# A sparse graph-attention kernel: masks only on slots that may be empty, one look at the sums per layer, and 272 slots in place of 277

## The chip, the cores and the metric

The kernel runs on one core of one Trainium2 chip. The metric is the device time in microseconds from the start to the end of one execution, as a median over several runs. A core has five engines that work through their own queues of instructions and wait for one another by semaphores: PE (TensorE, matrix products; its weight loads are shown apart as PEld), DVE (VectorE, elementwise work and reductions), ACT (ScalarE, activations and copies), POOL (GpSimd, here mostly the issue of indirect DMAs) and SP (here plain DMAs). Sixteen DMA engines carry out the transfers.

## The reference

Four layers of graph attention work on the same graph: 2048 nodes, 8 batches, 128 features. The adjacency matrix is random with a density of 1/128, so a node has 16 neighbours in the mean. Cut to what matters:

```python
x = normal((8, 2048, 128)); adj = bernoulli(0.0078125, (2048, 2048))

# layers 0 and 1, 8 heads of 16
scores = einsum('bnhd,bmhd->bhnm', Q, K) / sqrt(16)
scores = where(adj == 0, -inf, scores)
attn_out = einsum('bhnm,bmhd->bnhd', softmax(scores), V)
x = layer_norm(h + attn_out @ Wo + bo)
x = layer_norm(x + relu(x @ W1 + b1) @ W2 + b2)

# layers 2 and 3
h = x @ W
e = leaky_relu((h @ a_src)[:, :, None] + (h @ a_dst)[:, None, :], 0.2)
att = softmax(where(adj == 0, -inf, e))
x = layer_norm(att @ h + x)
```

All of it is in float32.

## The kernel before

**Tiles and slots.** The kernel does not compute the 2048 x 2048 scores. On the chip it finds each node's list of neighbours, ranks the nodes by falling degree, and cuts the ranked nodes into 16 blocks of 128, one node per partition. Block t has a fixed number of slots, `CAPS[t]` (line 41): slot s of a block holds, for each of its 128 nodes, that node's s-th neighbour. Since the nodes are ranked, block 0 needs many slots and block 15 few. Block 0 has `BASE` = 28 ordinary slots and `FOLD` = 2 folded ones: in a folded slot the 128 partitions serve the first `MANY` = 16 nodes eight times over, so these 16 nodes have 28 + 16 slots. The caps sum to 277. A node that has fewer neighbours than its block has slots leaves some of its slots empty; an empty slot's index points at row 2048 of the table, which a gather skips in layers 0 and 1 (out of bounds) and reads as a row of zeros in layers 2 and 3.

**A layer.** The rows of a table in HBM hold, per node, the keys and values of all batches (layers 0 and 1, 8 KB) or the projected features and two exponentials per batch (layers 2 and 3, 4160 bytes). For each slot POOL issues one indirect gather of 128 rows (`gather`, L284). Slots are worked on in chunks: of up to two slots in layers 0 and 1, up to four in layers 2 and 3. `pieces` (line 63) cuts the blocks into chunks evenly and sets their order; seven buffers hold chunks, and `fetch` issues the gathers of a chunk four or five chunks ahead of the one in work.

**A chunk of layers 0 and 1** (`attention_chunk`) goes through these steps. DVE multiplies the gathered keys by the queries (L600) and adds pairs of products (L606). PE turns the sums round with eight transposes that accumulate in PSUM (L291, tile `pair`), so that slots and heads lie on partitions. For each slot, one more matmul adds the mask (L613): its stationary operand is the column of `lmask` for that slot, broadcast to 64 columns, which holds -1e30 for nodes where the slot is empty and 0 elsewhere; its moving operand is a bfloat16 identity. ACT takes the exponential (L620) into one of eight places of `ring`. PE turns the weights back (L624), ACT copies them (L628), DVE multiplies the values by them (L636), and PE adds the products into `acc` by transposing them (L291, tile `acc`), eight matmuls per slot.

**Sums of weights.** When a block's last chunk is through the exponential, `block_sums` adds all its exponentials by matmuls (L580), ACT copies the result (L585, tile `sums`, 128 x 64) and takes its logarithm, from which the scale of the block's output is made. The `sums` function then has DVE reduce the copy to its least and greatest value (L648, L649), into `dmin` and `dmax`, one column per layer and block.

**Tails.** After a block's last chunk its tail runs beside the next block's chunks: output projection, two layer norms, the feed-forward network, and the projection into the next layer's table (L688 to L731, L488), all on PE and ACT. The blocks get shorter towards the end of a layer while a tail stays the same.

**A chunk of layers 2 and 3** (`gat_chunk`) multiplies small vectors for the weights (L764, L765, L770), scales seven of eight batches of features on DVE (L776) and the eighth on ACT (L781), in layer 2 adds one pair of slots on DVE (L787), and adds up on PE (L291). It uses no mask: an empty slot's row is zero.

**Order of the work.** The program is written under a manual schedule: `layers` walks over the list of chunks and calls the steps of neighbouring chunks in a fixed interleaving (a chunk's value product comes up to three chunks after its key product), and generators in `threads` and `tails` are advanced between them. Each engine runs its queue in that order.

**The check at the end.** `find_lists` (L325 to L366) makes the lists, `lmask`, and one number per node in `over`: the entry just past the block's last slot (L340), which is zero if all neighbours fitted. `verdict` reduces `dmin`, `dmax`, `over` and the scores of layers 2 and 3 to one flag. If a neighbour list did not fit, or sums were out of range, the flag makes the program run `general_path` after it, a dense computation of all four layers. The profile of the kernel before shows no instruction of that path.

The functions that the diff touches:

Of the kernel before, what the change touches and what calls it, by code (L numbers as in the profile page):

```python
# [8 lines left out]
F32 = mybir.dt.float32  # L9
# [5 lines left out]
ALU = mybir.AluOpType  # L15
AX = mybir.AxisListType
# [20 lines left out]

BASE, MANY, FOLD = 28, 16, 2  # L40
CAPS = [BASE + FOLD, 23, 21, 20, 19, 18, 18, 17, 16, 16, 15, 14, 14, 13, 12, 11]

# [41 lines left out]
def sparse_path(ctx: ExitStack, tc: tile.TileContext, ins: dict, out: bass.AP, flag: bass.AP):  # L86
# [81 lines left out]
    found = dram.tile([N, N // SEG * 8], F32, name="found")  # L168
    dmin = const.tile([P, 4, NT], F32, name="dmin")
    dmax = const.tile([P, 4, NT], F32, name="dmax")  # L170

# [148 lines left out]
    def find_lists(t):  # L322

        every = work.tile([P, N // SEG * 8], F32, tag="cand", name="cand", bufs=3)
        nc.gpsimd.indirect_dma_start(  # L325
            out=every, out_offset=None, in_=found,
            in_offset=bass.IndirectOffsetOnAxis(ap=perm[:, t : t + 1], axis=0),
        )
        for _ in range(12):
            yield  # L330
        s = CAPS[t] if t > 0 else BASE + FOLD * (P // MANY)
        rounds = s // 8 + 1
        top = small.tile([P, 48], F32, tag="top", name="top")
        for r in range(rounds):
            nc.vector.max(top[:, 8 * r : 8 * r + 8], every)
            if r + 1 < rounds:
                nc.vector.match_replace(every, top[:, 8 * r : 8 * r + 8], every, 0.0)
            if r % 3 == 2:
                yield
        nc.vector.tensor_copy(over[:, 1, t : t + 1], top[:, s : s + 1])  # L340
        if t == 0:
            few = small.tile([P, 1], F32, tag="few", name="few", bufs=1)
            nc.vector.tensor_single_scalar(few, node[:, 0:1], float(MANY), op=ALU.is_ge)
            nc.vector.scalar_tensor_tensor(
                over[:, 1, 0:1], top[:, BASE : BASE + 1], few, over[:, 1, 0:1],
                op0=ALU.mult, op1=ALU.max,
            )
            pf = misc()[:, : s - BASE]
            nc.tensor.matmul(pf, spread, top[:, BASE:s], start=True, stop=True)
            own = small.tile([P, P // MANY, FOLD], F32, tag="own", name="own", bufs=1)  # L350
            nc.vector.tensor_mul(
                own, pf.rearrange("p (g i) -> p g i", i=FOLD),
                group[:, :, None].to_broadcast([P, P // MANY, FOLD]),
            )
            s = CAPS[0]
            nc.vector.tensor_reduce(
                top[:, BASE:s], own.rearrange("p g i -> p i g"), axis=AX.X, op=ALU.add
            )
        sl = slice(first[t], first[t] + s)
        nc.vector.tensor_scalar(lmask[:, sl], top[:, :s], 0.0, NEG, op0=ALU.is_equal, op1=ALU.mult)  # L360

        far = small.tile([P, 48], F32, tag="far", name="far")
        nc.vector.tensor_scalar(
            far[:, :s], top[:, :s], 0.0, float(N + 1), op0=ALU.is_equal, op1=ALU.mult
        )
        nc.vector.scalar_tensor_tensor(  # L366
            lists[:, sl], top[:, :s], -1.0, far[:, :s], op0=ALU.add, op1=ALU.add
        )
        yield
# [200 lines left out]
    def block_sums(l, t, box, last):  # L570

        assert written[0] - box["exps"][0][2] < RING
        terms = [(e, fold_slots[: e.shape[0], :]) for e, folded, _ in box["exps"] if not folded]
        if "partial" in box:
            terms.append((ident, box["partial"]))
        if last and t == 0:
            terms += [(merge, box["wf"][:, i, :]) for i in range(FOLD)]
        ps = misc()[:, : NB * NH]
        for i, (a, b) in enumerate(terms):
            nc.tensor.matmul(  # L580
                ps, a, b, start=i == 0, stop=i + 1 == len(terms), skip_group_check=True
            )
        name = "sums" if last else "partial"
        box[name] = small.tile([P, NB * NH], F32, tag=name, name=name)
        nc.scalar.copy(box[name], ps)  # L585
        box["exps"].clear()
        if last:
            box["r"] = small.tile([P, NB * NH], F32, tag="logs", name="logs", bufs=1)
            nc.scalar.activation(box["r"], ps, AF.Ln)
            threads.append(scales(l, box))  # L590

    def attention_chunk(l, c):
# [17 lines left out]
        for j in range(NH):  # L610
            turn_into(sc, hk[:, j, :], j == 0)
        for i in range(ns):
            nc.tensor.matmul(  # L613
                sc[i * NB * NH : (i + 1) * NB * NH, :],
                lmask[:, at + i : at + i + 1].to_broadcast([P, NB * NH]), ident_bf,
                start=False, stop=True, skip_group_check=True,
            )
# [27 lines left out]

    def sums(l, t, box):
        if l < 2:
            nc.vector.tensor_reduce(dmin[:, l, t : t + 1], box["sums"], axis=AX.X, op=ALU.min)  # L648
            nc.vector.tensor_reduce(dmax[:, l, t : t + 1], box["sums"], axis=AX.X, op=ALU.max)  # L649
            return  # L650
        box["r"] = reciprocal_sums(l, t, box["w"], NB, box.get("folded"))

# [1111 lines left out]
```

## Time and profile before

| | |
|---|---|
| median of 3 runs | 2881.68 us (2877.71 to 2886.89) |
| profiled execution | 2878.0 us, of which the span from first to last instruction is 2876.1 us |
| mean granted TensorE clock | 0.94 of full speed |
| finding lists and the first table | 0 to 150 us |
| layer 0 | 150 to 1165 us |
| layer 1 | 1165 to about 1955 us |
| layer 2 | to about 2435 us |
| layer 3 | to the end |
| HBM | 937.16 MB read, 91.55 MB written |
| gathers (L284) | 1108, of 277 slots in four layers |
| masks (L613) | 554, of 277 slots in two layers |
| chunks | 142 in layers 0 and 1 each, 75 in layers 2 and 3 each |

The profile shows one execution. A group of instructions is shown as: line, engine, operation, the tile written and the tiles read, shapes, how often; then, after a bar, the busy time in us and the mean duration in ns; after a second bar, how long the engine stood idle just ahead of these instructions and what ended that idle time. "DVE ... <-ACT weights L628" says that DVE waited until ACT's instruction of line 628 had written `weights`. A table of stretches gives, for each stretch of the span, the busy time and the number of instructions of each engine, then the granted TensorE clock, the mean busy share of the 16 DMA engines and the GB/s that they moved. In a timeline a row is: start in us, busy us, engine, line, and how many instructions were merged into it.

### The profile page before, as it was taken

How to read it: one execution, taken by the hardware profiler on the slowest of the kernel's cores; microseconds unless marked ns; L12 is line 12 of the kernel's file. 1: busy time of each engine (PE TensorE's matmuls, PEld its weight loads, DVE VectorE, ACT ScalarE, POOL GpSimd, SP SyncE). 2: the span in 40 equal slices, each digit the busy share in tenths (PEclk: the TensorE clock that was granted, in tenths of full speed). 3: DMA queues.
4: the chain of work that ended last, by engine and by line, in shares of the span. 5: the costliest groups of instructions: out<-in, count | busy, mean ns of one | idle time of the engine just before them, and what ended most of it. 6: DMA issues, size and time to landing. Idle time of an engine off the chain costs nothing.

```text
span 2876.1 us, 51147 instructions
## 1 busy us (share of the span) xinstructions
PE 2456.2 (85%) x18834; PEld 2217.1 (77%) x18834; DVE 2559.8 (89%) x2563; ACT 1383.4 (48%) x5035; POOL 1778.6 (62%) x1297
## 2 busy tenths in 40 slices
PE   5867899899999999699989999998577787787786
PEld 4656788788888888688888888887567786777786
DVE  8888999999999888899899999996889997698996
ACT  3511444454455554154444555556345565354454
POOL 1267688688657544655566565553777775577773
PEclk9978999999999999899999999999789888999998
DMA  9698899999989878789899999976999998899995
GB/s 359 247 367 326 351 332 350 367 329 348 378 322 359 296 278 350 269 313 349 336 371 357 349 362 354 335 285 222 355 411 400 407 405 333 307 411 412 411 412 210
DMA packets 200684, 987.57 MB, mean 343 GB/s; under 512 B 31916, under 2 KB 33708, under 8 KB 128432
## 3 DMA queue, kind: packets, MB, share of 16 engines
q0 software_dynamic: 175024, 890.45, 80.6%
q1 hardware_dynamic: 20502, 75.52, 6.8%
q10 hardware_dynamic: 4900, 18.24, 1.6%
q8 instruction: 152, 2.49, 0.3%
q14 instruction: 106, 0.87, 0.1%
HBM read 937.16 MB, written 91.55 MB: 358 GB/s over the span
## 4 chain that ended last, share of the span: by engine, by line
PE 47%; DVE 22%; DMA 11%; issue 8%; ACT 6%; POOL 1%; POOLq 0%; DVEq 0%; ACTq 0%
PE acc L291 16%; DMA kv<-table,lists 8%; DVE kv L600 7%; DVE kv L636 7%; PE pair L291 4%; PE m L731 4%; PE m L710 4%; PE m L488 3%; PE m L298 3%; DVE kv L776 2%; DMA kv<-table,sorted_lists 2%; PE m L726 2%; PE m L580 2%; PE m L539 2%; DVE kv L606 2%
## 5 line engine op out<-in xcount | busy, mean ns | idle before, releaser
L284 POOL DMA_INDIRECT kv<-table,lists x955 | 1324.0, 1386 | 685.8 <-PE acc L291 303.3
L291 PE MATMUL acc<-ident,kv 128*128 128x128 f32 x8208 | 1080.9, 286 | 157.7 <-DVE kv L636 71.1
L291 PEld LDWEIGHTS acc<-ident,kv 128*128 128x128 f32 x8208 | 981.2, 148 | 220.6 <-DVE kv L636 81.9
L600 DVE TENSOR_TENSOR kv<-kv,q 128x2048 f32<-128x2048 f32 (+1 forms) x282 | 628.9, 2230 | 59.6 <-DMA kv<-table,lists 28.3
L636 DVE TENSOR_TENSOR kv<-kv,weights 128x2048 f32<-128x2048 f32 (+1 forms) x284 | 636.9, 2242 | 47.5 <-ACT weights L628 47.5
L776 DVE TENSOR_TENSOR kv<-kv,pair 128x3584 f32<-128x3584 f32 (+1 forms) x150 | 540.0, 3600 | 1.0
L291 PE MATMUL pair<-ident,kv 128*128 128x128 f32 (+1 forms) x2272 | 303.6, 278 | 79.5 <-issue 58.5
L606 DVE TENSOR_TENSOR kv<-kv 128x1024 f32<-128x1024 f32 (+1 forms) x284 | 340.3, 1198 | 9.2
L291 PEld LDWEIGHTS pair<-ident,kv 128*128 128x128 f32 (+1 forms) x2272 | 260.2, 142 | 97.6 <-issue 71.9
L781 ACT ACTIVATE kv<-kv,ws 128x128 f32<-128x128 f32 x554 | 177.6, 397 | 174.7 <-DVE ws L770 169.7
L284 POOL DMA_INDIRECT kv<-table,sorted_lists x153 | 190.4, 1244 | 109.2 <-PE pair L624 27.6
L628 ACT COPY weights<-pair 128x128 f32<-128x128 f32 (+1 forms) x284 | 74.0, 261 | 381.4 <-PE pair L624 376.6
L451 ACT ACTIVATE n<-m,eps 128x128 f32<-128x128 f32 x512 | 181.1, 371 | 149.1 <-PE m L731 145.9
L620 ACT ACTIVATE ring<-pair 128x128 f32<-128x128 f32 (+1 forms) x284 | 78.1, 275 | 343.9 <-PE pair L613 343.0
L818 ACT ACTIVATE n<-m,eps 128x128 f32<-128x128 f32 x256 | 90.6, 372 | 174.3 <-PE m L810 172.0
L475 POOL DMA_INDIRECT table<-rows,perm x57 | 89.4, 1568 | 123.0 <-issue 26.7
L731 PE MATMUL m<-w_L_w,hT 128*128 128x128 f32 x1024 | 156.2, 275 | 0.0
L458 ACT ACTIVATE n<-m,rs 128x128 f32<-128x128 f32 x512 | 145.9, 374 | 0.1
L710 PE MATMUL m<-n1T,w_L_gnn_W 128*128 128x512 f32 x256 | 133.8, 606 | 3.2 <-ACT hT L715 3.2
L731 PEld LDWEIGHTS m<-w_L_w,hT 128*128 128x128 f32 x1024 | 134.9, 192 | 0.0
L488 PE MATMUL m<-w_L_h,xT 128*128 128x130 f32 x512 | 83.6, 295 | 42.3 <-ACT xT L462 26.8
L298 PE MATMUL m<-ident,n 128*128 128x128 f32 x640 | 110.3, 289 | 10.4 <-ACT scale L675 5.4
(217 smaller groups left out, 3770.5 us busy)
## 6 DMA issues: line engine op xcount, KB each, us to landing
kept<-xT SPq DMA_DIRECT2D x48, 512.0 KB, 6.7
xT<-kept SPq DMA_DIRECT2D x48, 512.0 KB, 7.4
kv<-in_adj_dram SPq DMA_DIRECT2D x16, 1024.0 KB, 10.8
table<-kv ACTq DMA_DIRECT2D x16, 1024.0 KB, 7.6
kv<-table,lists POOLq DMA_INDIRECT x955, 8.8
kv<-in_x_nodes_dram SPq DMA_DIRECT2D x16, 512.0 KB, 13.9
kv<-table,sorted_lists POOLq DMA_INDIRECT x153, 7.7
found<-cand POOLq DMA_DIRECT2D x16, 64.0 KB, 4.8
```

The lines of the kernel that those rows point to most:

```text
L284: nc.gpsimd.indirect_dma_start(out=dst, out_offset=None, in_=tables[l][:, :], in_offset=bass.IndirectOffsetOnAxis(ap=index, axis=0), bound ...
L291: nc.tensor.matmul(dst, src, ident, start=start, stop=True, is_transpose=True, skip_group_check=True)
L298: nc.tensor.transpose(pt[:, j * P : (j + 1) * P], src[:, j, :], ident)
L451: nc.scalar.activation(dst[:, i, :], z[:, i, :], AF.Square, bias=eps, scale=D**-0.5, accum_out=ss[:, i : i + 1],)
L488: nc.tensor.matmul(pp[:, j, :], xT[:, h + j, :], w["qkv"][:, D:] if l < 2 else w["h"], start=j == 0, stop=True, skip_group_check=True,)
L600: nc.vector.tensor_mul(kk, kk, q[:, None].to_broadcast([P, ns, NB, D]))
L606: nc.vector.tensor_add(hk.rearrange("p j (c h) -> p c j h", h=NH), kj[:, :, :NH, :], kj[:, :, NH:, :])
L636: nc.vector.tensor_mul(vv, vv, w.rearrange("p (s b h) -> p (s b) h", b=NB, h=NH)[:, :, None, :] .to_broadcast([P, ns * NB, HD, NH]),)
L710: nc.tensor.matmul(ph, wt["1"][:, f * P : (f + 1) * P], n1T.rearrange("p b c -> p (b c)"), start=True, stop=True,)
L731: nc.tensor.matmul(y[:, j, :], hT[:, f, j, :], wt["2"][:, f, :], start=False, stop=f == 1, skip_group_check=True,)
L776: nc.vector.tensor_mul(hv[:, :, :nv, :], hv[:, :, :nv, :], wc[:, :, :nv, None].to_broadcast([P, ns, nv, D]))
L781: nc.scalar.mul(hv[:, i, b, :], hv[:, i, b, :], ws[:, i, b - nv : b - nv + 1])
```

## The change

Three edits go together.

1. **Fewer slots.** `BASE` goes from 28 to 27, and blocks 6, 9, 12 and 15 lose one slot each: 277 slots become 272. Of a node past the sixteenth, at most 27 neighbours now fit.
2. **Masks only where a slot may be empty.** A new list `SURE` gives for each block a number of slots that every node of the block is taken to fill (22 in block 0, 10 in block 14, 0 in block 15; 233 in all). `attention_chunk` leaves out the mask's matmul for those slots; the folded chunk keeps its masks. `find_lists` checks it on the chip: if a node's entry in slot `SURE[t]` - 1 is zero, a 1 goes into `over`, and the flag is set. For this, fifteen of the sixteen plain copies of L340 become a step with a comparison and a maximum.
3. **Sums looked at once per layer.** ACT copies a block's sums into its part of one tile `block_sum` (128 x 16 x 64) in place of a tile of its own, and in layers 0 and 1 DVE reduces all 1024 values of a partition once, after the last block, to one column of `dmin` and `dmax`. The other columns are set to 1 at the start of the program by two memsets.

```diff
--- before.py
+++ after.py
@@ -37,8 +37,10 @@
 
 
 
-BASE, MANY, FOLD = 28, 16, 2
-CAPS = [BASE + FOLD, 23, 21, 20, 19, 18, 18, 17, 16, 16, 15, 14, 14, 13, 12, 11]
+BASE, MANY, FOLD = 27, 16, 2
+CAPS = [BASE + FOLD, 23, 21, 20, 19, 18, 17, 17, 16, 15, 15, 14, 13, 13, 12, 10]
+
+SURE = [22, 20, 19, 18, 17, 17, 16, 15, 15, 14, 14, 13, 12, 11, 10, 0]
 
 
 
@@ -168,6 +170,9 @@
     found = dram.tile([N, N // SEG * 8], F32, name="found")
     dmin = const.tile([P, 4, NT], F32, name="dmin")
     dmax = const.tile([P, 4, NT], F32, name="dmax")
+    nc.vector.memset(dmin[:, :2, :], 1.0)
+    nc.vector.memset(dmax[:, :2, :], 1.0)
+    block_sum = const.tile([P, NT, NB * NH], F32, name="block_sum")
 
 
 
@@ -337,7 +342,13 @@
                 nc.vector.match_replace(every, top[:, 8 * r : 8 * r + 8], every, 0.0)
             if r % 3 == 2:
                 yield
-        nc.vector.tensor_copy(over[:, 1, t : t + 1], top[:, s : s + 1])
+        if SURE[t] > 0:
+            nc.vector.scalar_tensor_tensor(
+                over[:, 1, t : t + 1], top[:, SURE[t] - 1 : SURE[t]], 0.0, top[:, s : s + 1],
+                op0=ALU.is_equal, op1=ALU.max,
+            )
+        else:
+            nc.vector.tensor_copy(over[:, 1, t : t + 1], top[:, s : s + 1])
         if t == 0:
             few = small.tile([P, 1], F32, tag="few", name="few", bufs=1)
             nc.vector.tensor_single_scalar(few, node[:, 0:1], float(MANY), op=ALU.is_ge)
@@ -580,9 +591,11 @@
             nc.tensor.matmul(
                 ps, a, b, start=i == 0, stop=i + 1 == len(terms), skip_group_check=True
             )
-        name = "sums" if last else "partial"
-        box[name] = small.tile([P, NB * NH], F32, tag=name, name=name)
-        nc.scalar.copy(box[name], ps)
+        if last:
+            nc.scalar.copy(block_sum[:, t, :], ps)
+        else:
+            box["partial"] = small.tile([P, NB * NH], F32, tag="partial", name="partial")
+            nc.scalar.copy(box["partial"], ps)
         box["exps"].clear()
         if last:
             box["r"] = small.tile([P, NB * NH], F32, tag="logs", name="logs", bufs=1)
@@ -610,6 +623,8 @@
         for j in range(NH):
             turn_into(sc, hk[:, j, :], j == 0)
         for i in range(ns):
+            if not c["folded"] and k + i < SURE[t]:
+                continue
             nc.tensor.matmul(
                 sc[i * NB * NH : (i + 1) * NB * NH, :],
                 lmask[:, at + i : at + i + 1].to_broadcast([P, NB * NH]), ident_bf,
@@ -645,8 +660,10 @@
 
     def sums(l, t, box):
         if l < 2:
-            nc.vector.tensor_reduce(dmin[:, l, t : t + 1], box["sums"], axis=AX.X, op=ALU.min)
-            nc.vector.tensor_reduce(dmax[:, l, t : t + 1], box["sums"], axis=AX.X, op=ALU.max)
+            if t == NT - 1:
+                every = block_sum.rearrange("p t c -> p (t c)")
+                nc.vector.tensor_reduce(dmin[:, l, :1], every, axis=AX.X, op=ALU.min)
+                nc.vector.tensor_reduce(dmax[:, l, :1], every, axis=AX.X, op=ALU.max)
             return
         box["r"] = reciprocal_sums(l, t, box["w"], NB, box.get("folded"))
 
```

## The prediction

> **What bounds the kernel now.** I read the busy shares of the page first, then the busy time by stage, then the groups of instructions by shape with the idle time ahead of each, and last the timeline of the weight loads around one mask.
>
> ```profile
> PE 2456.2 (85%) x18834; PEld 2217.1 (77%) x18834; DVE 2559.8 (89%) x2563; ACT 1383.4 (48%) x5035; POOL 1778.6 (62%) x1297
> ```
>
> DVE and PE are both close to full, so an average names no bound. The stages do (columns: stretch, its length, busy PE, PEld, DVE, ACT, POOL, then clock, DMA share, GB/s):
>
> ```profile
> 150.00:800.00 650.00, 563.79 (x4296) 499.46 (x4296) 603.12 (x498) 263.29 (x897) 481.89 (x297) 0.95 0.92 349
> 800.00:1150.00 350.00, 340.73 (x2643) 300.19 (x2642) 305.49 (x219) 193.28 (x666) 192.11 (x114) 1.00 0.85 324
> 1165.00:1700.00 535.00, 485.87 (x3817) 434.38 (x3818) 502.19 (x301) 239.08 (x895) 316.81 (x182) 0.96 0.90 344
> 1700.00:1960.00 260.00, 254.78 (x2071) 227.63 (x2070) 235.70 (x156) 150.97 (x575) 149.30 (x89) 1.00 0.86 323
> 2040.00:2435.00 395.00, 304.08 (x2260) 287.08 (x2260) 368.88 (x430) 220.37 (x877) 283.24 (x262) 0.88 1.00 394
> 2435.00:2876.00 441.00, 342.59 (x2828) 331.90 (x2828) 361.44 (x440) 205.92 (x809) 284.80 (x279) 0.92 0.90 358
> ```
>
> Layer 0 is the first two rows, layer 1 the next two, layers 2 and 3 the last two. In both attention layers the first part has DVE at 93 to 94% (DVE-tight); in the last part, where the short blocks bring their tails closer together, PE is at 97 to 98% and DVE falls to 87 to 91% (PE-tight). Layer 2 has DVE at 93% with DMA at its full share; layer 3 is looser and waits for transfers.
>
> ```profile
> L636 DVE TENSOR_TENSOR kv<-kv,weights 128x2048 f32<-128x2048 f32 x270 | 619.8, 2296 | 47.5 <-ACT weights L628 47.5
> L600 DVE TENSOR_TENSOR kv<-kv,q 128x2048 f32<-128x2048 f32 x268 | 611.9, 2283 | 59.6 <-DMA kv<-table,lists 28.3 <-ACT q L544 19.3 <-DMA kv<-table,sorted_lists 10.6
> L606 DVE TENSOR_TENSOR kv<-kv 128x1024 f32<-128x1024 f32 x270 | 330.5, 1224 | 8.7
> L636 DVE TENSOR_TENSOR kv<-kv,weights 128x1024 f32<-128x1024 f32 x14 | 17.0, 1214 | 0.0
> L648 DVE TENSOR_REDUCE dmin<-sums 128x1 f32<-128x64 f32 x32 | 6.9, 215 | 20.7 <-ACT sums L585 20.5
> L649 DVE TENSOR_REDUCE dmax<-sums 128x1 f32<-128x64 f32 x32 | 6.7, 208 | 0.0
> L776 DVE TENSOR_TENSOR kv<-kv,pair 128x3584 f32<-128x3584 f32 x106 | 412.0, 3886 | 0.8
> L776 DVE TENSOR_TENSOR kv<-kv,pair 128x2688 f32<-128x2688 f32 x42 | 124.0, 2953 | 0.2
> ```
>
> The last column is what DVE lost ahead of each group. The 47.5 us for weights and the 20.5 us for sums both end on ACT copies of PE results: they are DVE waiting for a late PE. By stage, 18.2 us (layer 0) and 11.8 us (layer 1) of the weights' wait and 19 us of the sums' wait lie in the PE-tight parts.
>
> ```profile
> 1611.95 0.91 PEld L291 LDWEIGHTS pair<-ident,kv 128*128 128x128 f32 x8
> 1613.02 0.11 PEld L613 LDWEIGHTS <-lmask 128*64 128x64 bf16 x2 [0.17 <-issue]
> 1613.20 0.86 PEld L291 LDWEIGHTS acc<-ident,kv 128*128 128x128 f32 x8
> ```
>
> Eight transposes load every 109 ns. Then PE stands for 0.17 us, loads two masks of 64 columns at the same moment, and only at 1613.20 goes on with 128 columns. Over the whole trace, the median from the end of the last transpose to the end of the first product after the masks is 434 ns (lower quartile; half the chunks lie between this and 0.8 us, with other waits in them), where undisturbed neighbours end 109 ns apart. A chunk with masks thus costs PE 0.325 us more than one without, with one mask (434 ns too) as with two.
>
> **What the Trainium skill says.** "TensorEngine Tiling (Array Packing)", Key Properties: changing the tiling mode drains TensorE, and tiles run in parallel. The trace agrees: the pauses stand on both sides of the 64-column masks, and the two loads coincide. "Perfetto Trace Analysis", Identifying the Most-Contended Engine: judge DVE by occupancy, PE by weight-load occupancy rather than matmul occupancy. Here PEld is at 86 to 88% in the PE-tight parts; the missing tenth is largely these pauses, so I call PE tight all the same. "VectorE: DVE Perf Modes", perf-mode tier table: a tensor_reduce has only the plain mode. The trace has one over 1024 f32 elements, at 1220 ns. "DMA: Bandwidth & Descriptors", Where 436 GB/s comes from, puts one core's share of HBM at about 358 GB/s; layer 2 moves 394 over 395 us, so I don't take that figure as a wall.
>
> **The change part by part.**
>
> *Masks.* 554 mask matmuls become 78: of 284 chunks, 56 keep a mask (counted by cutting the blocks as the code does). 228 x 0.325 = 74 us of PE time go. Only the PE-tight parts turn that into time: they hold 53 + 40 = 93 chunks (starts of L600 in those windows), 80% lose their masks, 75 x 0.325 = 24 us. In the DVE-tight parts (103 + 89 chunks) DVE covers it; what shows there is a shorter wait for weights. It is 1.2 + 16.3 us there; I take half, 9 us, with 0 and 17.5 as ends.
>
> *Slots, layers 0 and 1.* Blocks 0, 6, 9, 12 and 15 lose one slot each. The built order shows 8 fewer two-slot chunks and 6 more one-slot chunks over both layers. A two-slot chunk is 2283 + 1224 + 2296 = 5.80 us of DVE, a one-slot chunk 1214 + 700 + 1214 = 3.13: 8 x 5.80 - 6 x 3.13 = 27.6 us. By chunk count, five of the ten slots lie in the DVE-tight parts, all of them two-to-one cuts: 5 x 2.67 = 13 us. In the PE-tight parts a slot is eight accumulating transposes: 5 x 8 x 0.109 = 4 us. The gathers bring nothing: POOL is at 62%, and a slot that is empty in all 128 rows fetches no row here (the 890 MB of POOL's queue fit the 32,733 edges of each layer at 8 KB, 277 x 128 rows at 4.16 KB in each of layers 2 and 3, and the scatters).
>
> *Slots, layers 2 and 3.* Each layer has five chunks cut from four slots to three: 5 x (3.886 - 2.953) = 4.7 us of DVE, and 5 x 0.53 MB, at 394 GB/s 6.8 us of transfer. DVE is nearly full in layer 2, DMA in places of layer 3: 5 us each, 10 together (6 to 14).
>
> *Sums.* 64 reductions at about 0.211 us go, 13.5 us; 36 of them are in the DVE-tight parts, 7.6 us. Four over 1024 elements at 1.22 us come, 4.9 us, and wait for ACT's copy of the last block. They stand at the ends of layers 0 and 1, where DVE idles 7.3 us and 11.4 us for the next layer's gathers: nothing, or +4.9 if that cover is gone. Queued behind them on DVE is the last chunk's L636 with the outputs after it; but the small reductions waited at the same place before (4.6 us at the end of layer 1), so no wait is new. The waits for sums in the PE-tight parts are PE's lateness and counted with it; 1 us goes in the rest.
>
> *The check.* A copy of 149 ns becomes a two-operand step of 220 ns (row of L405) fifteen times, +1.1 us, and block 9 saves one round of maximum and replacement, -0.6: 0. The two memsets at the start lie in DVE's 1.95 us wait for the identity; uncovered, some 0.1 us each by the row of a like memset. Fetching ranks loses one POOL gather of 1.6 us, off the path. SP's queue and the order of steps stay.
>
> Sum: PE-tight 24 + 4 = 28; DVE-tight 13 + 8 + 9 + 1 = 31; layers 2 and 3 10; together 69 to 70 us. The profiled execution took 2878.0 us (span 2876.1), so it would take 2808. The median of the runs shown, 2881.68, is 3.7 above it: 2812.
>
> **Rivals.**
> *Transfers take the place.* Bytes of layers 0 and 1 don't fall, the share is already 0.90 to 0.92 in the DVE-tight parts, and single stretches of 50 us reach 0.98. If the fuller half of these parts can't shrink, 15 of the 31 us are lost: 2827; with queueing in the PE-tight parts too, up to 2840. For it: DVE waits 28.3 us for gathers of L600. Against: most of that is in the first 150 us of layer 0, and gathers run four to five chunks ahead.
> *PE's pause hides elsewhere.* If the instruction after the masks would have waited anyway, only work counts: 4 + 13 + 8 + 10 = 35 us, 2847. For it: upper quartile of 0.8 us. Against: lower quartile and median nearly equal.
> *More comes back.* If relieving PE ends all its waits, DVE's side decides in the PE-tight parts: 14 us of slots, 5.5 of reductions and some 45 of idle time, 64 in place of 28. Half of that excess, and the full 17.5 us of waits, give 2881.7 - 70 - 18 - 8 = 2786.
> *Slower: the dense path.* The check can set the flag that runs the general path after the sparse one. It decides at a single row with fewer neighbours than SURE for its block, or a node past the sixteenth with more than 27. Counted from the inputs, the least degree equals SURE in ten blocks and the largest past the sixteenth is 27: met with nothing to spare. Its price: at least 256 x 4 score matmuls of 512 columns at 0.606 us (row of L710) per batch and attention layer, 16 times 0.62 ms, so over 12,000 us.
>
> **How the numbers follow.** Forecast 0.58 (its own range 2796 to 2828), transfers 0.15, hidden pause 0.12, more back 0.10, dense path 0.02, and 0.03 that gain and new waits cancel. A measurement tells about 0.3%, 8.6 us, from no change: faster 0.95, same 0.03, slower 0.02. The range 2783 to 2848 takes in the three near rivals; what is left out is the last two cases and the tails.
>
> **What would show it.** L613 at 78, with weight loads back to back after most transposes; L648 over 1024 elements, four in all; waits for weights and sums well below 47.5 and 20.5 us; DVE at 94% or more in the first parts of layers 0 and 1, and these layers shorter by 25 to 35 us each. Wrong, if waits of L600 for gathers grow by more than 10 us, or if PE stays at 97% with the layers no shorter.

## The result and the profile after

The changed kernel takes 2842.29 us in the median of five runs (2836.66 to 2843.96); the kernel before took 2881.68 us in five runs beside it. The ratio is 0.9861, with a 95% interval of 0.9842 to 0.9881: 39 us less, where the forecast said 70. The time lies in the range.

The profiled execution after took 2843.96 us (span 2842.2 us). Its busy times, from the head of the page:

```profile
PE 2388.3 (84%) x18176; PEld 2180.7 (77%) x18176; DVE 2520.0 (89%) x2496; ACT 1375.9 (48%) x5021; POOL 1753.6 (62%) x1276
```

PE lost 67.9 us of busy time and DVE 39.8 us. The work went away as forecast, but it did not all come back as time. The same stretches as in the prediction, after (length, busy PE, PEld, DVE, ACT, POOL, clock, DMA share, GB/s):

```profile
150.00:800.00 650.00, 554.87 (x4149) 500.76 (x4148) 598.82 (x480) 266.81 (x914) 479.31 (x295) 0.93 0.92 351
800.00:1150.00 350.00, 325.74 (x2533) 292.30 (x2531) 302.27 (x205) 190.07 (x653) 185.03 (x116) 0.99 0.85 325
1165.00:1700.00 535.00, 485.61 (x3829) 442.39 (x3828) 506.12 (x292) 252.98 (x961) 314.72 (x183) 0.96 0.92 352
1700.00:1960.00 260.00, 243.90 (x1947) 220.89 (x1946) 222.84 (x142) 156.33 (x588) 144.49 (x89) 0.99 0.83 309
```

In the second and fourth row PE is now at 93 to 94% and DVE at 86%: nobody is full. These windows have slipped by up to 35 us against the work, so the next pair is cut at the same work instead: blocks 10 to 14 of layer 1, from the first key product of block 10 to that of block 15. Before:

```profile
1692.00:1908.00 216.00, 211.26 (x1730) 189.58 (x1730) 200.72 (x127) 123.52 (x469) 126.65 (x74) 1.00 0.91 340
```

After:

```profile
1661.00:1876.00 215.00, 203.55 (x1661) 185.68 (x1660) 195.44 (x117) 122.34 (x470) 127.89 (x74) 1.00 0.91 346
```

PE lost 7.7 us of work here and DVE 5.3 us, and the stretch is 1 us shorter; from block 10 to the start of block 14 it takes 175.8 us before and 175.2 us after. What took the place is in DVE's waits in these two windows (total, times, longest). Before:

```profile
DVE kv L636 <- ACT weights L628: 9.0, 5, 3.2
DVE dmin L648 <- ACT sums L585: 4.9, 3, 1.8
```

After:

```profile
DVE kv L651 <- ACT weights L643: 18.3, 11, 4.1
```

The wait that the forecast wanted to see shrink has grown. The groups by shape over the whole trace after (busy and mean ns, then idle time ahead of them):

```profile
L651 DVE TENSOR_TENSOR kv<-kv,weights 128x2048 f32<-128x2048 f32 x262 | 601.4, 2296 | 50.1 <-ACT weights L643 50.0
L613 DVE TENSOR_TENSOR kv<-kv,q 128x2048 f32<-128x2048 f32 x260 | 593.7, 2283 | 55.2 <-DMA kv<-table,lists 35.9 <-ACT q L555 12.8 <-DMA kv<-table,sorted_lists 4.5
L651 DVE TENSOR_TENSOR kv<-kv,weights 128x1024 f32<-128x1024 f32 x20 | 24.6, 1232 | 11.0 <-ACT weights L643 11.0
L628 PE MATMUL pair<-ident_bf,lmask 128*64 128x128 bf16 x78 | 13.9, 247 | 0.0
L665 DVE TENSOR_REDUCE dmin<-block_sum 128x1 f32<-128x1024 f32 x2 | 2.4, 1220 | 7.1 <-ACT block_sum L595 7.1
```

The counts are those of the forecast: 78 masks, 8 fewer two-slot chunks, four large reductions at 1.22 us (two of each kind). The waits are not: for weights and sums DVE lost 47.5 + 20.5 = 68.0 us before and 50.0 + 11.0 + 7.1 = 68.1 us after. For gathers by `lists` ahead of the key product it lost 28.3 us before and 35.9 us after, for those by `sorted_lists` 10.6 and 4.5 us.

Between the ends of the transposes of an unmasked chunk and of the product behind them, PE's lower quartile fell from 434 to 109 ns. The timeline of weight loads after shows such a chunk, with transposes of `acc` before and behind a back transpose:

```profile
1816.69 0.91 PEld L296 LDWEIGHTS acc<-ident,kv 128*128 128x128 f32 x8
...
1817.56 0.14 PEld L639 LDWEIGHTS pair<-ident,ring 128*128 128x128 f32 x1
...
1817.67 0.90 PEld L296 LDWEIGHTS acc<-ident,kv 128*128 128x128 f32 x8
```

So the price of a pause was right where nothing else holds PE up. It is not so everywhere: the upper quartile of the same distance is 0.80 us before and 1.04 us after. The lead of the changed kernel, read at the first DVE instruction of a block in both traces, gives where time came from: 17.7 us at the start of layer 1 (its first key product stands at 1058.5 us before, so the row from 800 to 1150 us holds the first chunks of layer 1 too), 35.1 us at the start of layer 2 (1954.4 against 1919.3 us), 40.4 us at the last DVE product (2865.6 against 2825.2 us). At the end of the span only 33.9 us of it is left; why is told under the slots below.

### The profile page after: what moved, and what is told of

Read it like the earlier page. It is cut to its first block, busy times and chain, and to the rows that moved or that the text cites. A ratio compares the mean times of both kernels' runs of the same rounds, so it can differ in the third digit from the quotient of the medians.

```text
span 2842.2 us, 49663 instructions
## 1 busy us (share of the span) xinstructions
PE 2388.3 (84%) x18176; PEld 2180.7 (77%) x18176; DVE 2520.0 (89%) x2496; ACT 1375.9 (48%) x5021; POOL 1753.6 (62%) x1276
## 4 chain that ended last, share of the span: by engine, by line
PE 43%; DVE 22%; DMA 15%; issue 8%; ACT 6%; POOL 1%; POOLq 0%; DVEq 0%; ACTq 0%
PE acc L296 15%; DMA kv<-table,lists 10%; DVE kv L613 7%; DVE kv L651 7%; PE pair L296 4%; PE m L748 4%; PE m L727 4%; DMA kv<-table,sorted_lists 3%; PE m L303 2%; PE m L499 2%; DVE kv L793 2%; PE m L591 2%; PE m L743 2%; DVE kv L619 2%; PE m L550 2%
## 5 line engine op out<-in xcount | busy, mean ns | idle before, releaser
L289 POOL DMA_INDIRECT kv<-table,lists x938 | 1301.2, 1387 | 672.4 <-PE acc L296 327.7
L296 PE MATMUL acc<-ident,kv 128*128 128x128 f32 x8048 | 1060.5, 286 | 171.6 <-DVE kv L651 87.8
L296 PEld LDWEIGHTS acc<-ident,kv 128*128 128x128 f32 x8048 | 964.4, 149 | 241.6 <-DVE kv L651 111.8
L651 DVE TENSOR_TENSOR kv<-kv,weights 128x2048 f32<-128x2048 f32 (+1 forms) x282 | 626.1, 2220 | 61.1 <-ACT weights L643 61.0
L613 DVE TENSOR_TENSOR kv<-kv,q 128x2048 f32<-128x2048 f32 (+1 forms) x280 | 618.0, 2207 | 55.2 <-DMA kv<-table,lists 35.9
L793 DVE TENSOR_TENSOR kv<-kv,pair 128x3584 f32<-128x3584 f32 (+1 forms) x150 | 530.7, 3538 | 0.9
```

Source lines behind the costliest of these rows:

```text
L289: nc.gpsimd.indirect_dma_start(out=dst, out_offset=None, in_=tables[l][:, :], in_offset=bass.IndirectOffsetOnAxis(ap=index, axis=0), bound ...
L296: nc.tensor.matmul(dst, src, ident, start=start, stop=True, is_transpose=True, skip_group_check=True)
L613: nc.vector.tensor_mul(kk, kk, q[:, None].to_broadcast([P, ns, NB, D]))
L651: nc.vector.tensor_mul(vv, vv, w.rearrange("p (s b h) -> p (s b) h", b=NB, h=NH)[:, :, None, :] .to_broadcast([P, ns * NB, HD, NH]),)
L793: nc.vector.tensor_mul(hv[:, :, :nv, :], hv[:, :, :nv, :], wc[:, :, :nv, None].to_broadcast([P, ns, nv, D]))
```

## The experiments

The runs were made on four chips. On two of them the kernel before takes 2882 us, as in the comparison above; on the other two (masks_alone, slots_alone, sums_alone and slots_sums on one, pause_moved on the other) it takes 3001.5 and 2998.7 us. No kernel was traced on both kinds of chip. But from block 10 to the end of layer 0 sums_alone takes 265.1 us, as the kernel before does on the faster chip, while from the start of layer 2 to the end it takes 1044 us against 922. So I take the difference to lie in layers 2 and 3. Besides the ratio, which is always against the kernel before on the same chip, I compare the time at which layer 2 starts. It comes from one trace each: the two traces of the changed kernel differ by 0.5 us there, and by up to 2 us at the starts of single blocks.

| kernel | ratio to before (95%) | layer 2 starts (us) |
|---|---|---|
| before | 1 | 1954.4 |
| the change | 0.9861 (0.9842 to 0.9881) | 1919.3 |
| the change again (full_again) | 0.9853 (0.9838 to 0.9868) | 1919.8 |
| masks_alone | 0.9911 (0.9894 to 0.9928) | 1935.7 |
| slots_alone | 0.9872 (0.9851 to 0.9893) | 1933.3 |
| sums_alone | 0.9983 (0.9963 to 1.0003) | 1958.3 |
| slots_sums | 0.9886 (0.9862 to 0.991) | 1939.0 |
| masks_and_slots | 0.9876 (0.9861 to 0.9891) | 1921.2 |
| late_order | 0.9845 (0.9831 to 0.9858) | 1923.0 |
| y_split | 0.9993 (0.9982 to 1.0003) | 1944.8 |
| scale_later | 0.9835 (0.9822 to 0.9849) | 1906.4 |
| pause_moved | 0.9933 (0.991 to 0.9956) | 1945.4 |
| act_less | one run, 2829.96 us | 1909.0 |
| pe_less | one run, 2769.24 us | 1847.9 |

### One part at a time

**masks_alone** is the kernel before with `SURE`, its check, and

```diff
+            if not c["folded"] and k + i < SURE[t]:
+                continue
```

> Of the three edits only the masks: left out on slots that every node of the block fills, with the check on the chip; 277 slots and small reductions as before. The trace after shows PE freed by some 70 us and DVE's waits for weights and sums unchanged in sum (68 us before, 61 plus 7 after), so theory A says that PE's pauses were not what DVE waited for: 0 to 8 us less than before. Theory B, the terms of the prediction (24 us in the PE-tight parts and 9 us of waits in the others): 30 to 35 us less. Theory C, that masks do return it when alone and lose it to fuller DMA queues only together with the other edits: also 30 us or so less here, and more than the difference between the full change and the two other edits.

Layer 2 starts 18.7 us earlier. From block 10 to the end of the layer it gave 5.5 us in layer 0 and 0.9 us in layer 1, together 6.4 of the forecast's 24 (6.6 over the very chunks of its two PE-tight stretches); the other 12 us came in the DVE-tight blocks. The claim that masks return nothing fell; the claim that they return what PE saves fell too. About a quarter of the 74 us came back, most of it outside the PE-tight blocks.

Two things make the 24 too large from the start. Blocks 10 to 15 lose the masks of 58 of their 82 chunks, since block 15 keeps all of its masks: 58 x 0.325 = 19 us. And the product behind the masks could not always use the time. From the end of a chunk's transposes to the end of that product PE takes 220.9 us over all 284 chunks before and 175.7 us with masks alone: 45 us less, not 74. In blocks 10 to 15 it is 11.4 us less, not 19. In 95 of the 226 chunks without masks the next product adds into `acc` and needs DVE's value product; over these the time stayed at 116 us.

**slots_alone** changes only `BASE` and `CAPS`.

> Only the slots: 272 in place of 277, all masked, small reductions as before. Theory A, DVE's side decides nearly everywhere: 27.6 us of DVE in layers 0 and 1 and some 9 in layers 2 and 3, less what stands in the turn from layer 1 to 2: 25 to 35 us less. Theory B, the terms of the prediction: 13 + 4 + 10 = 27 us less; it does not tell the two apart here, but fixes what is left for the other edits. Theory C: as B.

Layer 2 starts 21.1 us earlier, where the forecast had 13 + 4. With block 12's lost slot, blocks 10 to 13 take 1.4 us longer in both layers; block 15's, which takes a whole chunk from the end of the layer, gave 6.5 us in layer 0 and 4.8 us in layer 1. The idle time ahead of DVE's value product tells why it is less than the 27.6 us of DVE work that go. With slots alone, and below it with masks alone:

```profile
L636 DVE TENSOR_TENSOR kv<-kv,weights 128x2048 f32<-128x2048 f32 (+1 forms) x282 | 626.2, 2221 | 57.4 <-ACT weights L628 46.7 <-ACT rs L441 5.4 <-ACT rs L442 4.5
L647 DVE TENSOR_TENSOR kv<-kv,weights 128x2048 f32<-128x2048 f32 (+1 forms) x284 | 637.0, 2243 | 39.1 <-ACT weights L639 26.7 <-ACT rs L450 9.7 <-issue 2.6
```

With slots alone DVE loses these 57.4 us and 19.0 us for sums, 8 us more than before: it comes sooner to the same late PE. With masks alone it is 39.1 and 18.0 us, 11 us less than before. Together the two nearly cancel.

This part also has a cost that the forecast did not have. The last scatter of results is followed by the program's closing. Here is POOL's last indirect DMA before, in a span of 2876.1 us:

```profile
2870.17 0.95 POOL L860 DMA_INDIRECT out_dram<-n,perm  x1 [11.81 <-DVEq L1759]
```

After, in a span of 2842.2 us:

```profile
2827.16 0.95 POOL L877 DMA_INDIRECT out_dram<-n,perm  x1 [9.24 <-DVE n L875]
```

From there to the end it is 5.9 us before and 15.0 us after. The trace's records of POOL's sequencer name it: the closing update of its DMA semaphore takes 0.36 us before and 2.06 us after, and the drain behind it 0.73 and 7.81 us. All three kernels with 277 slots have the short pair and all eleven traces with 272 slots the long one (within 0.14 us), on chips of both kinds. 2.6 us are won just ahead of it, where the last scatter follows the start of the last DVE product by 2.0 us in place of 4.6. The net is 6.5 us lost. The number of POOL's indirect DMAs (1264 and 1243) is what differs; why the closing depends on it is open.

**sums_alone** changes only the copy into `block_sum`, the reductions and the memsets.

> Only the sums: 64 small reductions replaced by four over 1024 elements. Theory A: the 13.5 us of reductions come back only where DVE is the pace; the 20.5 us of waits for sums turn into waits for weights, so 4 to 9 us less. Theory B: 9 us less. If the wait for sums itself was the loss (rival), 9 + 15 = 24 us less.

Layer 2 starts 3.9 us later, where the forecast had a gain of 8. The times of whole runs show no loss (ratio 0.9983, 0.9963 to 1.0003), so what is shown is that the gain didn't come. Its groups show why:

```profile
L641 DVE TENSOR_TENSOR kv<-kv,weights 128x2048 f32<-128x2048 f32 (+1 forms) x284 | 637.9, 2246 | 63.9 <-ACT weights L633 43.9 <-ACT rs L444 10.7 <-ACT rs L445 6.6
```

Most of the waits for sums (20.5 us before, 6.6 us here) are gone with the small reductions, and the idle time ahead of the value product rose from 47.5 to 63.9 us. A small reduction stood on DVE just ahead of a value product that waited for the same late PE, so it had filled a wait. And in layer 0 the waits for gathers rose from 28.3 to 33.8 us.

**slots_sums** and **masks_and_slots** leave out one part each.

> The full change without its masks part: 272 slots, all masked, sums looked at once per layer. Theory A: as fast as the full change within 8 us, about 2845 to 2850 us. Theory B: 33 us slower than the full change, about 2875 us. Theory C: about as fast as the full change too, but then masks alone must show its 30 us.

> The full change without the sums part: 272 slots, masks left out, small reductions per block as before. Theory E (additive): 19 + 21 = 40 us less up to layer 2, which begins at about 1915 us, 4 us ahead of the full change, since the sums part loses 4. The prediction's term: the sums part gains 9 us, so 9 us slower than the full change. Rival: the sums part's loss stands only next to the masks of before, and the two are equal.

Slots and sums start layer 2 15.4 us earlier, where their own runs add up to 17.2; masks on top of them are worth 19.7, as alone. Masks and slots without sums start it 33.2 us earlier, where 39.8 would be the sum; so in their presence the sums' part gains 2 us (4.7 us in the medians on one chip, 2845.48 against 2840.76) rather than loses 4. The three parts alone add up to 18.7 + 21.1 - 3.9 = 35.9, against 35.1 measured. The parts add, with a few us of interplay.

### Where the rest of PE's time went

**late_order** moves the ranking of layer 2's lists, and with it 50 small gathers on POOL, from blocks 2 and 6 to blocks 6 and 10. It tests whether transfers held the gain back.

```diff
-                    if t in (2, 6):
-                        threads.append(order_lists(t // 4))
+                    if t in (6, 10):
+                        threads.append(order_lists(t // 10))
```

> The full change with the small rank gathers of the two sorted lists begun at blocks 6 and 10 of layer 0 in place of 2 and 6. In layer 0 of the full change DVE waits some 36 us for gathers, more than the 28 us of before, and POOL is busy 84% between 400 and 500 us. Theory F, POOL's rank gathers hold up the large ones: the waits between 400 and 520 us (6 us) go and layer 0 is 3 to 8 us shorter, unless they come back later. Rival, DMA bandwidth sets these waits: no change within 2 us in layer 0.

DVE's waits between 324 and 571 us, after:

```profile
DVE kv L613 <- DMA kv<-table,lists: 7.1, 8, 2.0
DVE kv L613 <- ACT q L555: 1.1, 1, 1.1
```

And in late_order:

```profile
DVE kv L613 <- ACT q L555: 3.6, 3, 2.0
DVE kv L651 <- ACT weights L643: 0.2, 1, 0.2
```

The waits for gathers are gone and blocks 2 to 5 are 9.3 us shorter. But blocks 6 to 9, which now hold the first list's small gathers in place of the second's, are 3.3 us longer, and blocks 10 to 13 8.7 us: the small gathers of one list cost some 9 us, in blocks 2 to 5 as in blocks 10 to 13. The growth of the gathers' wait is real, and moving its cause doesn't recover it.

**y_split** does the second feed-forward product of a tail in two steps in place of one, with the same instructions, so that a chunk's back transpose waits behind half of it.

```diff
+            if j == 1:
+                yield
```

> The full change with the second feed-forward product of a tail (3 us of PE in one piece) cut into two pieces with a step of the interleaving between them. In the full change DVE still waits 61 us for weights, mostly where that piece stands ahead of a chunk's back transpose in PE's queue. Theory G, such pieces in PE's order set the pace of the last blocks, not PE's load: waits for weights fall by 10 to 25 us and layers 0 and 1 together by 5 to 15 us. Rival, PE's load sets it: no change, since the work is the same. Second rival: the tail gets longer by a step, and the turns between layers lose some 2 us each.

The whole gain is lost: 2880.98 us. No product was added. Of the three theories the second rival had the direction right, and far too small a size. The wait for weights is 81.3 us where the changed kernel has 61.1:

```profile
L651 DVE TENSOR_TENSOR kv<-kv,weights 128x2048 f32<-128x2048 f32 (+1 forms) x282 | 626.0, 2220 | 81.3 <-ACT weights L643 81.0
```

Halving what stands ahead of the back transpose did not help, and a step more shifts every later step of the tail by one. The order of the steps is worth 25 us by the start of layer 2, as much as a third of the masks' PE time, and PE's busy time doesn't tell it. Another 12 us are lost behind that point, where DVE's waits for the gathers of layers 2 and 3 are 92.8 us in place of 79.4.

**The loop behind it.** The slow chunks are those in which a tail's work stands in PE's queue ahead of the back transpose. In the trace after, 26 of DVE's waits for weights are over 1 us, 52.5 of the 61.1 us in all; in 23 of these, matmuls of the second feed-forward product stand in the 3 us ahead of the back transpose. Here is one in layer 1, the first chunk of block 13, in the timeline of the kernel before:

```profile
1834.39 0.27 PE L624 MATMUL pair<-ident,ring 128*128 128x128 f32 x1
...
1836.63 1.12 ACT L458 ACTIVATE n<-m,rs 128x128 f32<-128x128 f32 x4
...
1836.94 0.24 PE L613 MATMUL pair<-ident_bf,lmask 128*64 128x128 bf16 x2
...
1837.80 0.42 PEld L298 LDWEIGHTS m<-ident,n 128*128 128x128 f32 x4 [0.27 <-ACT n L458]
...
1842.58 0.27 PE L624 MATMUL pair<-ident,ring 128*128 128x128 f32 x1
...
1843.63 2.29 DVE L636 TENSOR_TENSOR kv<-kv,weights 128x2048 f32<-128x2048 f32 x1 [2.09 <-ACT weights L628]
```

The same chunk after (the chunk ahead of it, whose back transpose is the first row, now has one slot in place of two):

```profile
1802.46 0.27 PE L639 MATMUL pair<-ident,ring 64*128 64x64 f32 x1
...
1803.79 1.06 ACT L681 ACTIVATE scale<-logs 128x1024 f32<-128x1024 f32 x1
1804.75 1.12 ACT L469 ACTIVATE n<-m,rs 128x128 f32<-128x128 f32 x4
...
1805.92 0.42 PEld L303 LDWEIGHTS m<-ident,n 128*128 128x128 f32 x4 [0.59 <-ACT n L469]
...
1810.70 0.27 PE L639 MATMUL pair<-ident,ring 128*128 128x128 f32 x1
...
1811.47 0.25 ACT L643 COPY weights<-pair 128x128 f32<-128x128 f32 x1
1811.76 2.29 DVE L651 TENSOR_TENSOR kv<-kv,weights 128x2048 f32<-128x2048 f32 x1 [4.05 <-ACT weights L643]
```

From one back transpose to the next it is 8.19 us before and 8.24 us after. Behind the masks PE has to transpose the tail's normalized rows `n`, which ACT scales behind the exponential of `scale`. ACT starts that scaling 2.24 us after the back transpose before and 2.29 us after, so PE goes on 3.41 and 3.46 us after it. Without the mask PE is there sooner and waits 0.59 us in place of 0.27: the saved 0.325 us turned into a wait. Then come 3 us of the feed-forward product, then the back transpose. DVE, which came sooner, has waited 4.05 us for it in place of 2.09.

**scale_later** takes ACT's exponential of `scale` out of this place, by starting that thread one step later.

```diff
-            threads.append(scales(l, box))
+            threads.append(later(1, lambda: scales(l, box)))
```

> The full change with the making of a block's output scale (ACT's exponential of L681, 1.06 us, and what follows) begun one step of the interleaving later. In the full change the slow chunks of the last blocks run round one loop: back transpose on PE (L639), then ACT's weights copy, sums copy, logarithm, scale and four row scalings of a tail in one queue, then PE's transposes of these rows and the 3 us product, then the next back transpose; 8.2 us in the kernel before and 8.1 us after, with no mask in it. Theory H, this loop and not PE's load sets the pace there: about 1 us less in each of some 14 to 30 blocks, so layers 0 and 1 together 10 to 25 us shorter. Rival P, PE's load sets it: no change. Second rival, from the run with the split product: any step that comes later makes the tail longer, and it gets slower by up to 20 us.

Layer 2 starts 13 us earlier than in the changed kernel, and DVE's wait for weights falls from 61.1 to 47.9 us:

```profile
L651 DVE TENSOR_TENSOR kv<-kv,weights 128x2048 f32<-128x2048 f32 (+1 forms) x282 | 626.4, 2221 | 47.9 <-ACT weights L643 47.8
```

The median is 2834.65 us, the lowest of all kernels that compute everything; in the ratios its interval still touches that of the change. It supports the loop, with a reserve: 8 of the 13 us came before block 10, where I had expected less.

**act_less** drops ACT's scaling of the normalized rows in the tails: ACT's busy time falls by 126 us. **pe_less** keeps one of the three products of the second feed-forward step: PE's busy time falls by 105.5 us, that of its weight loads by 112.9. Each is a single run, and its output is another.

> The full change without the four row scalings on ACT in each layer norm of layers 0 and 1 (1.5 us of ACT 128 times; the rows go on as the squares that ACT wrote before, so the output is another). PE's work is the same. Theory H: the last blocks of both layers (from block 10 on) get shorter by 15 to 40 us together. Rival P: within 3 us, since ACT is only 55 to 60% busy there.

> The full change with the second feed-forward product of layers 0 and 1 cut to a third (no residual and only one half of the hidden rows, so the output is another): eight of twelve matmuls go, 1.8 us of PE in each of 64 half tiles, some 50 us of it from block 10 on. Both theories expect a gain here; its size tells the yield: rival P, PE's load sets the pace: 40 to 50 us from block 10 on. Theory H, the piece lies in the loop, but DVE takes over as soon as the loop is shorter than its own 5.7 us per chunk: 20 to 35 us from block 10 on, and nearly nothing in the blocks before.

The 126 us of ACT are worth 10.2 us, 8 of them from block 10 on, where theory H had 15 to 40: ACT is a link of the loop, not the bound. The 113 us of PE are worth 71.4 us, 63%, and DVE's wait for weights nearly ends:

```profile
L651 DVE TENSOR_TENSOR kv<-kv,weights 128x2048 f32<-128x2048 f32 (+1 forms) x282 | 626.4, 2221 | 10.3 <-ACT weights L643 10.3
```

So PE's lateness is what DVE waits for, and PE time can be worth a lot; this piece stands right ahead of the back transpose. From block 10 on 364 of its 1024 matmuls go, some 40 us at 0.109 us each (an estimate from the distance of undisturbed loads), and 38.2 us came, between the ranges of H and P: there a product taken out is worth nearly its whole time, which speaks for PE's load (rival P). That nearly none of the gain would come before block 10 was wrong; 33 us did.

**pause_moved** is the changed kernel with mask products issued for all chunks just ahead of the back transpose. They add nothing to the result that is used; they put a pause on PE at another place of each chunk. There it is paid in full: the median from the end of the product ahead to the end of the back transpose is 435 ns in place of 110, 89 us in all.

> The full change with the masks' matmuls put back for all 282 chunks at another place: after the exponential has read the scores, just ahead of the chunk's back transpose (L639), where their result goes unused, so the output stays the same. PE gets the pause of 0.325 us per chunk that the change took away, 92 us in all; masks at their old place in 228 chunks cost 19 us up to layer 2 (masks alone against before), which would be 23 us for 282. Theory Q, a pause costs what PE's load costs wherever it stands: 20 to 26 us more up to layer 2. Theory H, what counts is PE's time ahead of the back transpose, as in the cut product (72 us for 114 us of PE, 63%): 40 to 60 us more, for the same PE time. Rival, PE has room now in these places: under 10 us.

Layer 2 starts 26 us later than in the changed kernel, 29% of the pauses, at the upper end of the 20 to 26 expected by theory Q, by which a pause counts at about a quarter wherever it stands in a chunk; theory H (40 to 60) failed. By block, though, the 26 us of pauses from block 10 on (80 chunks at 0.325 us) cost 19 us (73%), and the 66 us before it cost 7. The masks at their old place gave back 6.4 us in those blocks, of 19 us of pauses or of the 11.4 us that PE gained there. That fits the loop (behind the masks PE waits for ACT, behind the back transpose DVE waits for PE), but the totals didn't separate the two places, so it is argued and not shown.

**full_again** repeats the changed kernel beside these runs.

> The full change once more, beside the others of this call, since the chip of the first four runs gave 3001 us for the kernel before, all of the difference in layers 2 and 3 (layers 0 and 1 took the same time on both to 0.5 us). By the traces up to layer 2's first block, masks alone bring 19 us, slots alone 21, sums alone lose 4, and the full change 35. If that adds up (theory E), the full change is at 0.984 to 0.988 of before here too, and layer 2 begins some 35 us earlier than before, at about 1919 us.

Ratio 0.9853; layer 2 starts at 1919.8 us. The starts of layers 1 and 2 repeat within 0.7 us.

## Why the prediction was right in direction and too high by 31 us

| step | forecast (us) | measured (us) |
|---|---|---|
| masks, blocks 10 to 15 | 24 | 6.4 |
| masks, earlier blocks (half of the waits for weights) | 9 | 12.2 |
| slots, layers 0 and 1 | 13 + 4 | 21.1 |
| sums | 8 + 1 | -3.9 alone, +2 beside masks and slots |
| layers 2 and 3 to the last product | 10 | 5.3 (40.4 - 35.1); 2.8 in full_again |
| closing of the program | 0 | -6.5 |

The measured rows, with sums at -3.9, add up to 34.6; the traces differ by 33.9 us and the medians by 39.4, since the profiled execution before was 3.7 us faster than its median and that after 1.7 us slower.

- *Masks.* The count (228 chunks) and the price of a pause (0.325 us) were right. The step that failed is "Only the PE-tight parts turn that into time", with "75 x 0.325 = 24 us": 6.4 us came. The 80% is the mean of all blocks; in blocks 10 to 15 only 58 chunks lose their masks, 19 us. Of these PE gained 11.4 us at the place, since the product behind often had to wait anyway, and 6.4 us reached the end. So a pause is not worth its length, though a product is worth nearly that in the same blocks (pe_less: 38.2 us for some 40).
- *The reading of PE.* The forecast read PE's 97 to 98% as the bound and set aside the weight loads' 86 to 88% with "the missing tenth is largely these pauses". They are about a third of it: its 53 and 40 pauses of 0.325 us are 17 of the 50 us and 13 of the 32 us that the weight loads leave free there. The Trainium skill, "Perfetto Trace Analysis", Identifying the Most-Contended Engine, says to judge PE by its FLOP utilization and its weight loads rather than by matmul occupancy. The trace agrees in that the weight loads showed room that the occupancy hid; what a removed piece returns neither figure tells. The rival that PE's pause hides elsewhere (35 us, 2847) was nearer than the forecast in size, and the wait that it named is the one seen behind the masks.
- *Half the waits for weights.* 9 us were taken for the DVE-tight parts, 12.2 came, in part by luck. With masks alone the waits for weights and sums before block 10 fell by 4 us only (27.1 to 22.9); more came in DVE's waits for `q`, which PE makes and ACT copies (19.3 to 10.0 us over layers 0 and 1). What the forecast missed is that the slots open the same waits again, so that in sum they stay at 68 us.
- *Slots.* 21.1 us came for 17. The PE-tight price of 0.9 us a slot missed block 15, where a whole chunk leaves the end of a layer and its chain. That the closing on POOL grows by 8.8 us could not be read from the kernel before.
- *Sums.* "36 of them are in the DVE-tight parts, 7.6 us" failed: DVE time just ahead of a wait of DVE itself was no gain. Of the large reductions, the forecast gave "nothing, or +4.9 if that cover is gone". In layer 0 it held (80.5 us from block 14 to the end in sums_alone, 80.4 before); in layer 1 they cost 2.0 us (88.2 against 86.2). DVE there, after:

```profile
1914.79 1.22 DVE L665 TENSOR_REDUCE dmin<-block_sum 128x1 f32<-128x1024 f32 x1 [4.59 <-ACT block_sum L595]
1915.93 1.21 DVE L666 TENSOR_REDUCE dmax<-block_sum 128x1 f32<-128x1024 f32 x1
1917.05 2.28 DVE L651 TENSOR_TENSOR kv<-kv,weights 128x2048 f32<-128x2048 f32 x1
1919.25 0.18 DVE L781 TENSOR_TENSOR kv<-kv,own 128x32 f32<-128x32 f32 x1
```

  The wait of 4.59 us is as long as before, but it comes ahead of the reductions. Behind them the last value product and layer 2 follow with no gap: the idle time for the next layer's gathers, which was to cover them, isn't there.
- *Transfers.* The first rival came in small: waits for gathers by `lists` grew by 7.6 us in layer 0, under the 10 us named as a sign of being wrong, and those by `sorted_lists` in layer 1 fell by 6.1. late_order shows that POOL's small gathers are part of the former.
- *Signs.* The counts and the shapes came. Not so the "waits for weights and sums well below 47.5 and 20.5 us" and layers 0 and 1 "shorter by 25 to 35 us each": the waits stayed, and the layers got 17.7 and 17.4 us shorter.
- *The dense path* did not run: no instruction of it is in the trace.

Still open: where the 5 us went that PE gained behind the scores in blocks 10 to 15 and that did not come back (the loop of the timeline is one place; how often it took them was not measured), and why scale_later brought 8 us before block 10, where PE isn't tight.

## What to carry to other kernels

Where two in-order engines are about equally busy, as here (84 and 89%), price a removed piece by what stands behind it in its queue: if the next instruction waits for another engine, the piece was filling a wait and returns a part of itself or nothing. Measure that at the place: here the pauses were priced at 74 us, PE gained 45 behind them, and 19 reached layer 2. Look for the place where DVE's long waits end (here the back transpose behind a tail's product) and shorten what stands right ahead of it; 113 us of weight loads there gave 71, and moving one exponential of another engine gave 13. Count the pieces in the stretch itself and not by the mean of the program. Before counting on an idle stretch as cover, look at which side of the new instruction its wait lies.

## What the runs showed of the hardware that I had not expected

- One mask of 64 columns costs PE as much as two: 434 ns against 109 between ends (lower quartiles). Ahead of the back transpose, where pause_moved put them, it is 435 ns against 110 in the median.
- POOL's closing drain is 7.67 to 7.81 us in the eleven traces with 1243 indirect DMAs and 0.73 us in the three with 1264.
- The same kernel took 2882 us on some chips and 3001.5 us on another. By the traces of its variants the difference lies in the layers with gathers of 4 KB rows: in layer 3 the fullest fortieths of the span move 412 GB/s before and 372 GB/s in sums_alone.
- One step more in the order of a tail, with the same instructions, costs 40 us (2840.76 to 2880.98 on the same chip).
